# Token-major x, causal row sums from VectorE blocks, and a layer norm folded behind W in an attention kernel

## The chip, the cores and the metric

The kernel runs on one core of one Trainium2 chip. Times are device microseconds (us) of that core. Most executions of one kernel agree within 0.3%. "PE" is TensorE, "PEld" its weight loads, "DVE" VectorE, "ACT" ScalarE, "POOL" GpSimd, "SP" SyncE, "SPq" the order of transfers that SyncE issues. All runs used below are of the fast state.

## The reference, cut to what matters

```python
x = x + conv_attention(group_norm(x))     # causal: q, k, v from x and positions; softmax; times v
t = tokens(x)                             # 8 images x 2304 tokens x 128 channels, fp32
t = t + softmax(xh @ xh.T) @ xh           # xh = layer_norm(t): full attention, scores symmetric
t = t + ffn(layer_norm(t))                # y = sigmoid(batch_norm(W x) + V y), token after token
```

## The kernel before

Each image has six chunks of 384 tokens. A chunk passes through causal attention, a layer norm, full attention, and a second layer norm whose result is multiplied by W; the recurrence runs at the end, for all images. Scores of the full attention are symmetric, so an exponential computed for one block serves for the mirrored one too. VectorE turns it in 32x32 squares into a tile `t`, SyncE stores it in memory as `e` (576 KB) and loads it back as `g` (four transfers of 144 KB), and the product `o<-g` uses it.

What stands behind the causal attention, with the row sums by three products of one column, and x transposed by TensorE:

```python
def sums():                                               # row sums of the causal softmax
    tp = psum_t(f"dn_{b}_{j}")
    for g in range(QB):                                   # QB = 3
        nc.tensor.matmul(tp[:, g : g + 1], acc[:, ts(g, P)], ones[:, 0:1], start=True, stop=True)
    nc.vector.reciprocal(ri, tp[:, :QB])
def residual():
    to = transposed(o_sb, f"oc_t_{b}_{j}")                # three 128x128 transposes by TensorE
    tx = transposed(xbuf[b][:, cols], f"x_t_{b}_{j}")
    nc.scalar.copy(xr, tx[:, :QC])
    ...                                                   # y = to * ri + xr
```

And behind the full attention, where t2 (the sum of the second line, tokens on partitions) is transposed once as it is and once normalized:

```python
(sums, residual, rooted,     # row sums, t2 = o * ri + t1, rs = 1/sigma by GpSimd
 keep,                       # tp = transposed(t2, "tk"), copied to t2c, stored for the end
 normed,                     # x2 = (t2 - mean) * rs       (VectorE)
 back,                       # xc = transposed(x2, "tx")
 statistics)                 # wx = W @ xc; batch-norm statistics
```

Loads of `g` run through three buffers; stores and loads stand in one order of issue, SyncE's.

Of the kernel before, what the change touches and what calls it, by code (L numbers as in the profile page):

```python
# [3 lines left out]

# [9 lines left out]
F32 = mybir.dt.float32  # L14
# [7 lines left out]
NPE = 2 * EMB  # L22
# [524 lines left out]
class Stream:  # L547
# [14 lines left out]
    def then(self, at, ops):  # L562

        for engine, us in ops:
            at = max(at + self.HOP, self.free[engine]) + us
            self.free[engine] = at
        return at + self.HOP
# [33 lines left out]
def fast_path(ctx: ExitStack, tc: tile.TileContext, x, wq, bq, wk, bk, wv, bv, w_ffn, v_ffn, gamma, beta, pe, out, flag):  # L601
# [28 lines left out]

    ident = cpool.tile([P, P], F32, tag="ident", name="ident")
    make_identity(nc, ident)
    ones = cpool.tile([P, P], F32, tag="ones", name="ones")
# [18 lines left out]
    with ExitStack() as actx:  # L652
# [40 lines left out]
        def load_x(b):  # L693
            xbuf[b] = big.tile([P, N], F32, tag="x", name=f"x_{b}")
            for h in range(2):
                nc.sync.dma_start(xbuf[b][:, ts(h, N // 2)], x_v[b, :, ts(h, N // 2)])

        load_x(0)


# [21 lines left out]
        wpT = chunk_tile("t2", "wpT").rearrange("p (j c) -> p j c", j=3)  # L722
        raw = tpool.tile([P, N // 2], F32, tag="t", name="raw")
        wn = [raw[:, ds(j * (C + NPE), C + NPE)] for j in range(3)]
        vn = raw[:, ds(3 * (C + NPE), P)]
        for j, (w, bias) in enumerate(((wq, bq), (wk, bk), (wv, bv))):
            nc.scalar.dma_start(wn[j], w)
            nc.scalar.dma_start(wpT[NPE : NPE + 1, j, :], bias.rearrange("(o c) -> o c", o=1))
            if j == 0:
                nc.scalar.dma_start(pe_sb[0][: NPE + 1, :], pe[:, : N // 2])  # L730
        nc.scalar.dma_start(pe_sb[1][: NPE + 1, :], pe[:, N // 2 :])
        nc.scalar.dma_start(w1, w_ffn)
        nc.scalar.dma_start(vn, v_ffn)
        nc.scalar.dma_start(gb[:, 0:1], gamma.rearrange("(c o) -> c o", o=1))
        nc.scalar.dma_start(gb[:, 1:2], beta.rearrange("(c o) -> c o", o=1))
        for j in range(3):
            tp = psum_t(f"tp_w_{j}")
            nc.tensor.transpose(tp[:, 0:P], wn[j][:, 0:C], ident)
            nc.tensor.transpose(tp[0:NPE, P : 2 * P], wn[j][:, C : C + NPE], ident)
            nc.vector.tensor_copy(wT[:, j, :], tp[:, 0:P])  # L740
            nc.vector.tensor_copy(wpT[0:NPE, j, :], tp[0:NPE, P : 2 * P])

        def ffn_weights():
            tp = psum_t("tp_ffn")
            nc.tensor.transpose(tp[:, 0:P], w1, ident)
            nc.tensor.transpose(tp[:, P : 2 * P], vn, ident)
            nc.vector.tensor_copy(w1T, tp[:, 0:P])
            nc.vector.tensor_copy(vT_f, tp[:, P : 2 * P])


        SQ = 32
        R = P // SQ
        same = apool.tile([P, R, SQ], F32, tag="same", name="same")
        nc.vector.tensor_reduce(same[:, 0, :], ident.rearrange("p (a c) -> p c a", c=SQ), AX.X, ALU.add)
        for r in range(1, R):
            nc.vector.tensor_copy(same[:, r, :], same[:, 0, :])
        mine = apool.tile([P, NQ - 1, R, QB], F32, tag="mine", name="mine")
        nc.vector.tensor_reduce(mine[:, 0, :, 0], ident.rearrange("p (a c) -> p a c", c=SQ), AX.X, ALU.add)
        for i in range(NQ - 1):
            for g in range(QB):  # L760
                if i + g:
                    nc.vector.tensor_copy(mine[:, i, :, g], mine[:, 0, :, 0])
# [45 lines left out]
        pos = {}  # L808

        def load_positions(b, n):  # L810
            if 0 < b < B:
                pos[b, n] = pbp.tile([P, 3, QC], F32, tag="pb", name=f"pb_{b}_{n}")
                nc.sync.dma_start(pos[b, n], posb_d[:, n])

        def project(b, n):
# [4 lines left out]
            def positions(j):  # L820
                def f():
                    if j == 0:
                        c["pb"] = pbp.tile([P, 3, QC], F32, tag="pb", name=f"pb_{b}_{n}")
                    pe_c = pe_sb[n // (NQ // 2)][: NPE + 1, ts(n % (NQ // 2), QC)]
                    ps = psum_s(f"pb_{n}_{j}")
                    if j < 2:
                        nc.tensor.matmul(ps[:, :QC], wpT[: NPE + 1, j, :], pe_c, start=True, stop=True)
                    else:
                        for m in range(0, QC, P):
                            nc.tensor.matmul(ps[:, ds(m, P)], pe_c[:, ds(m, P)], wpT[: NPE + 1, j, :], start=True, stop=True)  # L830
                    nc.scalar.copy(c["pb"][:, j, :], ps[:, :QC])
                    if j == 2:
                        nc.sync.dma_start(posb_d[:, n], c["pb"])

                return f

            def normed():
                if b:
                    c["pb"] = pos.pop((b, n))
# [5 lines left out]
                c["xn"] = chunk_tile("xn", f"xn_{b}_{n}", c, 4 if b else 7)  # L845
                nc.vector.tensor_scalar(c["xn"], xbuf[b][:, cols], mg, rs, ALU.subtract, ALU.mult)

            def part(j):
                def f():
# [14 lines left out]
                    if j < 2:  # L864
                        nc.vector.tensor_reduce(
                            largest[b][:, j, n : n + 1], dst, AX.X, ALU.max, apply_absolute_value=True
                        )
                    else:
                        load_positions(*divmod(b * NQ + n + 2, NQ))
                        if n + 1 < EARLY:  # L870
                            project(b, n + 1)

                return f

            steps = [] if b else [(positions(j), QC * US, [("ACT", 0.5)]) for j in range(3)]
            steps.append((normed, 0.0, [("DVE", 0.75)]))
# [31 lines left out]
        def transposed(src, name):  # L908
            tp = psum_t(name)
            for g in range(QB):  # L910
                nc.tensor.transpose(tp[:, ts(g, P)], src[:, ts(g, P)], ident)  # L911
            return tp

# [5 lines left out]
        class Causal:  # L919
# [57 lines left out]
            def after(self, j, o):  # L977
# [4 lines left out]
                o_sb = chunk_tile("o", f"oc_{b}_{j}", c, 2)  # L982
                nc.scalar.copy(o_sb, o[:, :QC])
                at = st.then(st.now, [("ACT", 0.5)])

                def sums():

                    tp = psum_t(f"dn_{b}_{j}")
                    for g in range(QB):
                        nc.tensor.matmul(tp[:, g : g + 1], acc[:, ts(g, P)], ones[:, 0:1], start=True, stop=True)  # L990
                    ri = small.tile([P, QB], F32, tag="ric", name=f"ric_{b}_{j}")
                    nc.vector.reciprocal(ri, tp[:, :QB])  # L992
                    c["ri"] = ri

                def residual():
                    to = transposed(o_sb, f"oc_t_{b}_{j}")
                    tx = transposed(xbuf[b][:, cols], f"x_t_{b}_{j}")
                    xr = chunk_tile("xr", f"xr_{b}_{j}", bufs=1)
                    nc.scalar.copy(xr, tx[:, :QC])  # L999
                    y = t1p.tile([P, QC], F32, tag="t1t", name=f"t1t_{b}_{j}")  # L1000
                    for g in range(QB):
                        nc.vector.scalar_tensor_tensor(  # L1002
                            y[:, ts(g, P)], to[:, ts(g, P)], c["ri"][:, g : g + 1], xr[:, ts(g, P)], ALU.mult, ALU.add
                        )
                    if j == NQ - 1 and b + 1 < B:
                        load_x(b + 1)
# [14 lines left out]
                def back():  # L1021
# [4 lines left out]
                    (sums, 0.6, [("DVE", 0.2)]),  # L1026
                    (residual, 0.7, [("ACT", 0.5), ("DVE", 2.6)]),
# [5 lines left out]
        class Full:  # L1033
# [3 lines left out]

            def __init__(self, b):
# [3 lines left out]
                self.used = 0  # L1042
# [23 lines left out]

            def prefetch(self):
                n = len(self.loaded)
# [4 lines left out]
            def turned(self, j, m, p, ready):  # L1073
# [3 lines left out]
                if g == 0:  # L1077
                    self.tiles[n] = tpool.tile([P, R, QB, QB, SQ], F32, tag="t", name=f"t_{b}_{j}_{n}")
# [5 lines left out]
                if g == QB - 1:  # L1084
                    d = dpool.tile([P, R, QB * QB * SQ], F32, tag=f"e_{j}_{n}", name=f"e_{b}_{j}_{n}")
                    nc.sync.dma_start(d, t.rearrange("p b j m r -> p b (j m r)"))
                    self.stored[j, n] = d, at
# [8 lines left out]
            def begin(self, j, what, first):  # L1096
# [12 lines left out]
                if what[0] == "turned":  # L1109
                    i, g = what[1:]  # L1110
                    while (i, j) not in self.loaded:
                        self.load()
# [24 lines left out]
            def after(self, j, o):  # L1137
# [5 lines left out]
                at = st.then(st.now, [("ACT", 0.5)])  # L1143

# [23 lines left out]
                def residual():  # L1168
                    tp = transposed(o_sb, f"of_t_{b}_{j}")
                    t2 = chunk_tile("t2", f"t2_{b}_{j}", c, 5)  # L1170
# [5 lines left out]
                    c["mv"], c["ve"] = moments(t2, f"f{b}_{j}", "l2")  # L1176

                def rooted():
                    c["rs"] = root(c["ve"], f"f{b}_{j}", "l2")

                def normed():
                    c["x2"] = chunk_tile("x2", f"x2_{b}_{j}", c, 6)
                    normalize(c["x2"], c["t2"], c["mv"], c["rs"])

                def keep():
                    tp = transposed(c["t2"], f"tk_{b}_{j}")
# [4 lines left out]
                    nc.scalar.copy(self.t2c[:, :, ds(s0, SJ)], tp[:, :QC].rearrange("p (s l) -> p l s", l=LS))  # L1191
# [6 lines left out]
                def back():  # L1198
                    tp = transposed(c["x2"], f"tx_{b}_{j}")
                    c["xc"] = chunk_tile("xc", f"xc_{b}_{j}", c, 7, bufs=1)  # L1200
                    nc.scalar.copy(c["xc"], tp[:, :QC])

                def statistics():
# [5 lines left out]
                c["chain"] = st.add([  # L1209
                    (sums, 0.15, [("DVE", 0.8)]),  # L1210
                    (residual, 0.35, [("DVE", 2.6)]),
                    (rooted, 0.0, [("POOL", 0.9)]),
                    (keep, 0.35, [("ACT", 0.5)]),
                    (normed, 0.0, [("DVE", 1.1)]),
# [197 lines left out]
```

## Time and profile before

The time before is 1854.35 us, the median of three runs (1854.31 to 1856.12).

| quantity | before | where it is read |
|---|---|---|
| span of the profiled run | 1852.4 us | head of the page |
| TensorE busy / idle | 1817.4 / 35.0 us | busy row; span less busy |
| mean granted TensorE clock | 0.993 | list of cores |
| DMA moved; share of SyncE's queue in 16 engines' time | 207.24 MB; 37.5% | DMA part |
| `e<-t` and `g<-e`, issue to landing (median) | 3.2 and 3.7 us | list of DMA issues |
| first score; first score of the full attention | 22.15; 130.16 us | TensorE in order of time |

The table is to be read as follows: TensorE has hardly any idle time left, and DMA has much. A queue's "share" adds up the time during which its packets were under way, on 16 engines. It counts waiting inside a packet like moving, and this will matter.

### The profile page before, as it was taken

How to read it: one execution, taken by the hardware profiler on the slowest of the kernel's cores; microseconds unless marked ns; L12 is line 12 of the kernel's file. 1: busy time of each engine (PE TensorE's matmuls, PEld its weight loads, DVE VectorE, ACT ScalarE, POOL GpSimd, SP SyncE). 2: the span in 40 equal slices, each digit the busy share in tenths (PEclk: the TensorE clock that was granted, in tenths of full speed). 3: DMA queues.
4: the chain of work that ended last, by engine and by line, in shares of the span. 5: the costliest groups of instructions: out<-in, count | busy, mean ns of one | idle time of the engine just before them, and what ended most of it. 6: DMA issues, size and time to landing. Idle time of an engine off the chain costs nothing.

```text
span 1852.4 us, 22328 instructions
## 1 busy us (share of the span) xinstructions
PE 1817.4 (98%) x6885; PEld 1159.6 (63%) x6886; DVE 1218.8 (66%) x3152; ACT 773.5 (42%) x1976; POOL 198.4 (11%) x292
## 2 busy tenths in 40 slices
PE   7999999999999999999999999999999999999987
PEld 4666666666666666666666666666666666666656
DVE  5747667575766667575675757666675756757457
ACT  2345334443345423454244433454234542445346
POOL 1100011000110001100110001100011000200006
PEclk9999999999999999999999999999999999999988
DMA  2105551256303571055511563034720456005667
GB/s 92 51 1 192 155 131 35 79 164 175 76 19 128 152 185 48 1 186 143 150 35 57 159 182 95 22 117 148 190 58 1 165 155 158 9 13 166 181 197 206
DMA packets 176558, 207.24 MB, mean 112 GB/s; under 512 B 85865, under 2 KB 147948, under 8 KB 175662
## 3 DMA queue, kind: packets, MB, share of 16 engines
q1 hardware_dynamic: 174608, 202.42, 37.5%
q0 software_dynamic: 720, 2.62, 0.9%
q8 instruction: 57, 0.93, 0.2%
q10 hardware_dynamic: 1102, 0.68, 0.1%
q14 instruction: 71, 0.58, 0.1%
HBM read 112.49 MB, written 93.19 MB: 111 GB/s over the span
## 4 chain that ended last, share of the span: by engine, by line
PE 96%; DVE 1%; POOL 1%; DMA 1%; issue 1%; ACT 0%; SPq 0%; POOLq 0%; DVEq 0%
PE s L1117 18%; PE o L1131 18%; PE s L948 16%; PE o L959 16%; PE o L1127 13%; PE pj L853 3%; PE pj L856 2%; PE wx L1205 2%; PE dn L990 1%; PE x_t L911 1%; PE tb L911 1%; PE of_t L911 1%; PE tx L911 1%; PE oc_t L911 1%; PE z L1346 1%; PE tk L911 1%
## 5 line engine op out<-in xcount | busy, mean ns | idle before, releaser
L1119 ACT ACTIVATE p<-s,shift 128x384 f32<-128x384 f32 x504 | 293.1, 582 | 448.5 <-PE s L1117 435.4
L1117 PE MATMUL s<-xh 128*128 128x384 f32 x1008 | 410.8, 489 | 0.0
L1131 PE MATMUL o<-p,xhT 128*128 128x384 f32 x1008 | 403.2, 487 | 0.0
L948 PE MATMUL s<-q,k 128*128 128x384 f32 (+2 forms) x1008 | 380.2, 459 | 0.5 <-DVE k L863 0.5
L959 PE MATMUL o<-p,vT 128*128 128x384 f32 (+2 forms) x1008 | 377.0, 456 | 0.0
L950 ACT ACTIVATE p<-s 128x384 f32<-128x384 f32 (+2 forms) x504 | 231.0, 462 | 349.6 <-PE s L948 287.4
L1127 PE MATMUL o<-g,xhT 128*128 128x384 f32 x720 | 279.7, 488 | 0.1
L1131 PEld LDWEIGHTS o<-p,xhT 128*128 128x128 f32 x1008 | 188.0, 190 | 121.3
L959 PEld LDWEIGHTS o<-p,vT 128*128 128x128 f32 x1008 | 188.5, 190 | 114.6 <-issue 0.3
L1117 PEld LDWEIGHTS s<-xh 128*128 128x128 f32 x1008 | 183.7, 190 | 106.8
L974 DVE TENSOR_TENSOR acc<-acc,p 128x384 f32<-128x384 f32 (+2 forms) x408 | 210.1, 515 | 60.0 <-ACT p L950 38.1
L948 PEld LDWEIGHTS s<-q,k 128*128 128x128 f32 x1008 | 178.6, 191 | 88.8 <-DVE acc L974 1.1
L1080 DVE STREAM_TRANSPOSE t<-p 128x384 f32<-128x384 f32 x360 | 187.0, 553 | 45.5 <-ACT p L1119 42.7
L1127 PEld LDWEIGHTS o<-g,xhT 128*128 128x128 f32 x720 | 132.2, 190 | 79.0 <-issue 0.7
L1090 DVE TENSOR_REDUCE tsum<-t 128x12 f32<-128x1152 f32 x120 | 162.3, 1353 | 4.1
L858 DVE TENSOR_TENSOR z<-pj,pb 128x384 f32<-128x384 f32 x144 | 79.2, 550 | 110.2 <-PE pj L853 105.3
L953 POOL TENSOR_TENSOR p<-p,triu 128x128 f32<-128x128 f32 x144 | 72.0, 500 | 447.3 <-ACT p L950 446.4
L901 POOL TENSOR_TENSOR rs_f<-ve_f,mhalf 128x3 f32<-128x3 f32 x48 | 41.5, 865 | 684.7 <-DVE ve_f L895 684.7
L992 DVE RECIPROCAL ric<-dn 128x3 f32<-128x3 f32 x48 | 8.5, 177 | 135.9 <-PE dn L990 135.9
L1119 ACT ACTIVATION_READ_ACCUMULATOR p<-s,shift 128x1 f32 x504 | 97.3, 193 | 0.0
L1002 DVE SCALAR_TENSOR_TENSOR t1t<-oc_t,ric,xr 128x128 f32<-128x128 f32 x144 | 41.6, 344 | 68.3 <-ACT xr L999 67.9
L853 PE MATMUL pj<-xn,wT 128*128 128x384 f32 x192 | 80.3, 504 | 0.0
(249 smaller groups left out, 1595.0 us busy)
## 6 DMA issues: line engine op xcount, KB each, us to landing
e<-t SPq DMA_DIRECT2D x120, 576.0 KB, 3.2
g<-e SPq DMA_DIRECT2D x480, 144.0 KB, 3.7
pb<-posb_d SPq DMA_DIRECT2D x42, 576.0 KB, 3.8
x<-in_x_dram SPq DMA_DIRECT2D x16, 576.0 KB, 4.8
out_dram<-t2s SPq DMA_DIRECT2D x26, 256.0 KB, 3.9
t_d<-t2c SPq DMA_DIRECT2D x16, 384.0 KB, 4.4
t2s<-t_d SPq DMA_DIRECT2D x6, 1024.0 KB, 6.9
posb_d<-pb SPq DMA_DIRECT2D x6, 576.0 KB, 2.8
```

The source lines that it names most:

```text
L853: nc.tensor.matmul(ps[:, :QC], wT[:, j, :], xn, start=True, stop=True)
L911: nc.tensor.transpose(tp[:, ts(g, P)], src[:, ts(g, P)], ident)
L948: nc.tensor.matmul(s[:, off:QC], keys[b][:, ts(m, P)], queries[b, j][:, off:], start=True, stop=True)
L950: nc.scalar.activation(p[:, off:], s[:, off:QC], AF.Exp, scale=SCALE)
L959: nc.tensor.matmul(o[:, off:QC], vals[b][:, ts(m, P)], p[:, off:], start=first, stop=last)
L974: nc.vector.tensor_add(a[:, off:], a[:, off:], p[:, off:])
L1080: nc.vector.transpose(t[:, :, :, g, :].rearrange("p b j r -> p j b r"), p.rearrange("p (j b r) -> p j b r", j=QB, b=R))
L1090: nc.vector.tensor_reduce(self.tsum[j][:, n - j - 1, :], t.rearrange("p b j m r -> p (b j) (m r)"), AX.X, ALU.add)
L1117: nc.tensor.matmul(s[:, :QC], xh[:, ts(m, P)], xh[:, ts(j, QC)], start=True, stop=True)
L1119: nc.scalar.activation(p, s[:, :QC], AF.Exp, bias=shift, accum_out=self.rows[:, m, j : j + 1])
L1127: nc.tensor.matmul(out_ap, xhT[:, QB * i + g, :], p, start=first, stop=last)
L1131: nc.tensor.matmul(o[:, :QC], xhT[:, what[1], :], p, start=first, stop=last)
```

## The change

The intent is to take work off TensorE. (1) The host also lays x token-major, so `x_t` goes. (2) VectorE transposes the sums in 32x32 squares and reduces them; one product of 12 columns and a mask finish the row sums. (3) W's rows are centred once, so the norm's mean falls out, and 1/sigma is multiplied on the product. Then only the raw t2 need be turned: VectorE turns its squares (`tt`), and a round trip through memory (`t2m`, `t2x`) puts the squares in place. 1/sigma, one number per token on the partition of that token, must become a row that every partition sees: it is written to memory (`rs`) and read back by all 128 partitions (`scale`). The last two chunks of the last image keep the old path. (4) Stores of `e` and these transfers are put in SyncE's order when their source is estimated to be ready. (5) The start gets idle products, host-laid weights and another order of positions. The diff, cut:

```diff
 def sums():                                    # causal
-    for g in range(QB):
-        nc.tensor.matmul(tp[:, g : g + 1], acc[:, ts(g, P)], ones[:, 0:1], start=True, stop=True)
+    nc.tensor.matmul(tp[:, :k], same..., c["parts"], start=True, stop=True)     # 12 columns
+    nc.vector.tensor_mul(own..., tp[:, :k], mine...)
+    nc.vector.tensor_reduce(ri, own.rearrange("p a g -> p g a"), AX.X, ALU.add)
 def residual():
-    tx = transposed(xbuf[b][:, cols], f"x_t_{b}_{j}")
...
+def spread():
+    c["rs_d"] = dpool.tile([QB, P], F32, tag=f"rs_{j % 2}", name=f"rs_{b}_{j}")
+    nc.sync.dma_start(c["rs_d"].rearrange("g p -> p g"), c["rs"])
+    c["t2_d"] = dpool.tile([P, QC], F32, tag=f"t2m_{j % 2}", name=f"t2m_{b}_{j}")
+    d = c["t2_d"].rearrange("(k c) (a f) -> a c k f", c=SQ, a=R)
+    for r in range(R):
+        nc.sync.dma_start(d[r], c["tt"][ts(r, SQ)].rearrange("c (k f) -> c k f", k=R))
+def fetch():
+    nc.sync.dma_start(c["t2x"], c["t2_d"])
+    nc.sync.dma_start(c["scale"], c["rs_d"].rearrange("g p -> (g p)").partition_broadcast(P))
+def product():                                  # wx = W' @ t2x, then times scale
...
+steps = [(spread, 0.0, [("", 10.0)]), (fetch, 0.0, [("", 9.0)]), (product, ...), (stored, ...)]
-    d = dpool.tile([P, R, QB * QB * SQ], F32, tag=f"e_{j}_{n}", name=f"e_{b}_{j}_{n}")
-    nc.sync.dma_start(d, t.rearrange("p b j m r -> p b (j m r)"))
+    self.to_store.append((j, n, t, at))         # stored later, when the estimate says ready
...
+for i in range(12):                             # idle products at the start
+    nc.tensor.matmul(tp[:, :P], ident, ident, start=True, stop=True)
```

Note the second line of `spread`. `rs` is a tile of 128 partitions x 3 numbers, and the target is laid out group by group. So each of the 384 numbers is a piece of 4 B of its own, and the pieces of neighbouring partitions lie side by side in memory. This transfer is called the scatter below.

## The prediction

> **What bounds the kernel now.** I read the head of the page, then the chain that ended last, then the order of time on TensorE inside one image, and last the waits.
>
> ```profile
> span 1852.4 us, 22328 instructions
> PE 1817.4 (98%) x6885; PEld 1159.6 (63%) x6886; DVE 1218.8 (66%) x3152; ACT 773.5 (42%) x1976; POOL 198.4 (11%) x292
> PE 96%; DVE 1%; POOL 1%; DMA 1%; issue 1%; ACT 0%; SPq 0%; POOLq 0%; DVEq 0%
> ```
>
> TensorE is busy for 1817.4 of 1852.4 us and carries 96% of the chain. The waits agree: from the second image to the seventh, TensorE waits for nothing longer than 0.3 us. The chain shows the same instruction once an image:
>
> ```profile
> 353.47 0.75 PE s L1117 x2
> 570.90 0.75 PE s L1117 x2
> ```
>
> So an image takes 217.43 us, all of it TensorE's instruction stream; the idle time (35.0 us in all) lies nearly all in the first 66 us (11.8) and after 1776 us. What counts is therefore how much room an instruction takes in that stream. This is read from start to start, because durations overlap. In order of time (start, duration, line):
>
> ```profile
> 1004.40 0.81 PE L1131 MATMUL o<-p,xhT 128*128 128x384 f32 x2
> 1005.04 0.72 PE L990 MATMUL dn<-ones,acc 128*128 128x1 f32 x6
> 1005.63 0.89 PE L1117 MATMUL s<-xh 128*128 128x384 f32 x2
> 1006.36 0.81 PE L1131 MATMUL o<-p,xhT 128*128 128x384 f32 x2
> 1007.00 0.49 PE L911 MATMUL oc_t<-ident,oc 128*128 128x128 f32 x3
> 1007.33 0.49 PE L911 MATMUL x_t<-ident,x 128*128 128x128 f32 x3
> 1007.66 0.81 PE L1117 MATMUL s<-xh 128*128 128x384 f32 x2
> ...
> 1033.37 0.33 PE L1153 MATMUL ts<-tsum,same 128*128 128x60 f32 x2
> 1033.53 0.87 PE L1117 MATMUL s<-xh 128*128 128x384 f32 x2
> 1034.23 0.81 PE L1131 MATMUL o<-p,xhT 128*128 128x384 f32 x2
> ```
>
> A product of 384 columns takes 0.645 us (1004.40 to 1005.04). A group of three transposes takes 0.33 us (1007.33 to 1007.66), though it is shown as 0.49. The row sums `dn` (three products with one column) take 0.59 us, and the product behind them 0.73 in place of 0.645, so 0.67 in all: three weight loads of a full block each for one column of output. One product of the kind `ts` takes 1034.23 - 1033.37 - 0.645 = 0.22 us.
>
> **What the Trainium skill says.** (1) "Perfetto Trace Analysis", Identifying the Most-Contended Engine, holds that matmul busy time is a poor measure of the distance to the roofline. True here too: the groups' own busy times add up to more than the engine's 1817.4 us. I use 98% only together with the absence of waits. (2) "TensorE: Matmul & The Clock Gate", Part 4, gives about 275 ns for a 128x128 transpose in a kernel. The trace has a mean of 273 to 277 ns, but its room in the stream is 0.33 / 3 = 0.11 us, and that is what a removed one returns. (3) "VectorE: DVE Perf Modes", The three transpose paths: VectorE transposes 32x32 blocks only. So the change has to finish the job with a small product and a mask (row sums) or with a transfer (t2). The trace's 128x384 stream transposes take 553 ns. (4) "DMA: Bandwidth & Descriptors", Specifications: transfers reach line rate from 512 B. The change writes t2 in pieces of 384 B and 1/sigma in pieces of 4 B. No line of before isolates that price.
>
> **The change, part by part.** The built programs of both kernels give the counts; there are 8 x 6 = 48 chunks.
>
> - Transposes. `x_t` goes (x now also comes token-major from memory): 48 groups. `tk` and `tx` go for all but the last two chunks, 46 each, because t2 is turned by VectorE and a transfer through memory, and the norm's mean goes into a centred W, its 1/sigma behind the product. 140 x 0.326 = 45.6 us less.
> - Row sums: 48 x 0.67 = 32.4 us go, 48 products of 12 columns come: 48 x 0.22 = 10.6. Net 21.8 us less.
> - Steady sum: 67.4 us. A middle image saves 6 x (3 x 0.326 + 0.67 - 0.22) = 8.6 us, so its period should be 208.9 us.
> - VectorE per chunk: + stream transpose of the sums 0.55, + reduction of 384 about 0.55 (`largest`, same size, 0.553), + mask and small reduction 0.33, + transpose of t2 0.55, + scaling out of PSUM 0.55, - normalization 3 x 0.29 = 0.87. That is +1.66 us, 79 us in all: 1219 becomes about 1295 us, 72% of the new span. Beside TensorE, not on its path.
> - ScalarE loses 48 copies of x_t at 0.48: 23 us less, off the path.
> - Transfers: per chunk 4 writes of 48 KB, a 1.5 KB scatter, and three reads of 192 KB (x, t2, the broadcast scale): 0.77 MB, so about 37 MB on 207. SyncE issues some 370 more (184 + 3 x 46 + 48 + 4). DMA share rises from 38% to perhaps 50%.
> - Start. Before, TensorE starts its first position product at 13.3 us and runs half as fast until about 22 us; the same four instructions:
>
> ```profile
> 13.32 2.92 PE L827 MATMUL pb<-pe,wpT 33*128 33x384 f32 x4
> 23.13 1.55 PE L827 MATMUL pb<-pe,wpT 33*128 33x384 f32 x4
> ```
>
> The first score is at 22.15 us. After, the weights need no transposes, 12 idle products warm the array, and two chunks of positions fill the group norm's wait. Adding the durations of the new order I get the first score at 14 to 16 us. Part of these 7 us is lost again: positions now go to memory and back through one free buffer before the third chunk's VectorE work (a store of 2.8 us and a load of 3.8, one after the other), and products wait for it. I count 4 us net, estimated between 0 and 8.
> - End. The last two chunks keep the old path, so the 77 us from the last `o` to the end should stay.
>
> Without new waits: 1854.35 - 67.4 - 4 = 1783 us.
>
> **The rivals.** (a) VectorE becomes the bound in places. Stretches of 10 us show where it has no room; the columns are the stretch, its length, and busy time of TensorE, its weight loads, VectorE, ScalarE, GpSimd, then clock, DMA share and GB/s:
>
> ```profile
> 1010.00:1020.00 10.00, 10.00 (x35) 5.98 (x34) 9.83 (x20) 5.71 (x17) 0.85 (x1) 1.00 0.74 255
> 1100.00:1110.00 10.00, 10.00 (x40) 6.28 (x39) 6.92 (x14) 2.83 (x8) 0.94 (x1) 1.00 0.99 240
> 1140.00:1150.00 10.00, 10.00 (x46) 6.98 (x45) 9.68 (x31) 3.75 (x9) 2.93 (x6) 1.00 0.17 45
> ```
>
> At 1010 and 1140 VectorE is over 96% busy, and the change adds 1 to 3 us of work there. Against it: just before 1010 VectorE sits idle for 5.3 us waiting for `dn` and 2.4 us for the copied x, and the new work fits into that; six buffers of p give several us of slack. If it bites: 1 to 2 us an image, 8 to 16 us.
> (b) Turned blocks come late. At 1100 DMA is already at 99%, and the loads of `g` run through three buffers:
>
> ```profile
> DMA to landing us min/median/max: 2.5/3.7/5.9
> ```
>
> Four issues (about 1.8 us) and 3.7 us of landing stand against roughly 6 us between a buffer's release and its next use. New stores of t2 and the scatter stand in SyncE's order ahead of such loads, and SyncE waits in order. For it: little slack. Against: before, no product waited for one, and the change places each transfer by an estimate. If it bites: 1 to 3 us an image, 8 to 25 us.
> (c) The round trip of t2 is longer than the 19 us that the schedule allows it, and TensorE waits at `wx`. Two landings of about 4 us stand against it, so I think it unlikely; it would cost some us an image.
> (d) The gain is hidden because something else ends last. The 96% of the chain speak against it.
>
> **Range and chances.** From 1783 I add 8 us for (a) and (b) together, about 1 us an image: 1791 us. If nothing waits and the whole start gain stays, 1854.35 - 67.4 - 8 = 1779; a little below that is possible. If (a) and (b) both bite hard (35 us), and the start gives nothing, 1787 + 35 = 1822; I think 1813 holds the upper tenth. A gain of over 2% needs 1817.3 us: 0.92. Within 2%: 0.06. Slower: 0.02, for a transfer that holds up SyncE's order every image.
>
> **What would show it.** Right: the period of a middle image near 209 to 210 us in the chain; no groups `x_t`, nearly none of `tk` and `tx`; `dn` as 48 small products; TensorE busy near 1750 us; VectorE near 1295; first score near 15 us. (a) would show as idle time of `s` or `o` ended by VectorE or by ScalarE waiting for VectorE; (b) as idle time of the products out of `g` ended by DMA; (c) as idle time of `wx` ended by the loads of t2x or scale. I am wrong if the period falls by clearly less than 8 us, or if the start up to the first full stage is not earlier than before.

## The result, and the profile after

The changed kernel took 1865.04 us (median of four runs, 1861.03 to 1866.10), beside 1854.51 us for the kernel before. The ratio is 1.0051, 95% interval 1.0033 to 1.0068: within 2%, and a little slower. (A ratio is the mean time of one kernel's fast runs over that of the other's fast runs in the same rounds, so it is not quite the ratio of the medians.) 1791 us had been predicted. Head, busy row and shares of the chain after:

```profile
span 1863.2 us, 21869 instructions
PE 1781.9 (96%) x6291; PEld 1106.2 (59%) x6291; DVE 1284.5 (69%) x3275; ACT 780.3 (42%) x1882; POOL 203.0 (11%) x303
...
PE 68%; DMA 16%; DVE 8%; issue 6%; SPq 1%; ACT 0%; POOL 0%; DVEq 0%; ACTq 0%; POOLq 0%
```

The work did go: TensorE has 594 fewer instructions. But it is busy for only 35.5 us less (1817.4 - 1781.9), and idle for 81.3 us instead of 35.0. The chain, which held 96% TensorE, now holds 16% DMA. TensorE's waits (what for: us in total, times, longest) name the transfer:

```profile
PE o L1170 <- DMA g<-e: 33.7, 23, 5.4
PE of_t L923 <- DVE t2x L1249: 10.0, 7, 3.4
...
PE o L1170 <- DMA t2m<-tt: 4.1, 2, 3.3
```

The turned blocks come late. One such place, first in SyncE's order of issue (start, how long the issue took, transfer):

```profile
452.48 0.38 SPq L1232 DMA_DIRECT2D rs<-rs_f  x1
453.10 2.28 SPq L1236 DMA_DIRECT2D t2m<-tt  x4
455.75 10.52 SPq L1094 DMA_DIRECT2D g<-e  x8
```

and then in TensorE's order of time (start, duration, instruction, and in brackets the idle time before it and what ended it):

```profile
456.53 0.81 PE L1170 MATMUL o<-g,xhT 128*128 128x384 f32 x2
462.76 1.62 PE L1170 MATMUL o<-g,xhT 128*128 128x384 f32 x2 [5.42 <-DMA g<-e]
464.17 1.49 PE L1160 MATMUL s<-xh 128*128 128x384 f32 x2
465.45 1.49 PE L1170 MATMUL o<-g,xhT 128*128 128x384 f32 x2
```

TensorE stands for 5.42 us, and then the next products take 1.28 us from start to start (465.45 - 464.17) instead of 0.645. After its idle time a stall is paid for a second time. The Trainium skill, "TensorE: Matmul & The Clock Gate", Part 1, says that an idle array falls to half its clock after an idle window of about 3.4 us and needs some busy microseconds to come back; this trace agrees, with 1.28 against 0.645 us. The chain at that place goes through two transfers (start, duration):

```profile
444.26 7.52 DMA e<-t
...
451.80 10.82 DMA g<-e
```

Before, they took 3.2 and 3.7 us at the median. The engines' share was high in these times, while few bytes moved. Windows of 10 us (busy times of TensorE, weight loads, VectorE, ScalarE, GpSimd, then clock, DMA share, GB/s) of the changed kernel, the first right after `rs` was issued at 390.05 us, the second after the one at 452.48:

```profile
390.00:400.00 10.00, 10.00 (x36) 6.11 (x35) 5.25 (x18) 4.25 (x14) 0.85 (x1) 1.00 0.93 109
...
460.00:470.00 10.00, 7.24 (x19) 4.36 (x20) 2.08 (x8) 0.67 (x2) 0.00 (x0) 0.66 0.78 164
```

At 390 us the 16 engines are 93% occupied with 109 GB/s. The kernel before moved 240 GB/s at 99% in the window from 1100 us that the prediction shows. So something keeps packets under way without moving bytes. DMA as a whole moved 246.23 MB (before 207.24), and SyncE's queue has a share of 58.5% (before 37.5%).

Theories after this reading. T1: the scatter `rs` of 4-byte pieces holds the engines. T2: the writes of t2 in 384-byte pieces do. T3: something else of the change does, such as later stores or more bytes. T4: not the engines but SyncE's order is the trouble, because it stands still at `rs` until GpSimd is done while loads of `g` queue up behind it.

### The profile page after: what moved, and what is told of

Same layout as the page of the kernel before. It is cut to its first block, busy times and chain, and to the rows that moved or that the text cites. A ratio compares the mean times of both kernels' runs of the same rounds, so it can differ in the third digit from the quotient of the medians.

```text
span 1863.2 us, 21869 instructions
## 1 busy us (share of the span) xinstructions
PE 1781.9 (96%) x6291; PEld 1106.2 (59%) x6291; DVE 1284.5 (69%) x3275; ACT 780.3 (42%) x1882; POOL 203.0 (11%) x303
## 2 busy tenths in 40 slices
DMA packets 241940, 246.23 MB, mean 132 GB/s; under 512 B 132913, under 2 KB 212690, under 8 KB 241044
## 3 DMA queue, kind: packets, MB, share of 16 engines
q1 hardware_dynamic: 240860, 241.73, 58.5%
## 4 chain that ended last, share of the span: by engine, by line
PE 68%; DMA 16%; DVE 8%; issue 6%; SPq 1%; ACT 0%; POOL 0%; DVEq 0%; ACTq 0%; POOLq 0%
PE o L983 14%; PE s L972 14%; PE s L1160 12%; PE o L1174 11%; PE o L1170 7%; DMA e<-t 6%; DMA g<-e 5%; PE pj L863 3%; DMA rs<-rs_f 2%; PE z L1457 1%; PE pj L866 1%; DVE t L1123 1%; PE tb L923 1%; DMA scale<-rs 1%; SPq L1094 1%
## 5 line engine op out<-in xcount | busy, mean ns | idle before, releaser
L1160 PE MATMUL s<-xh 128*128 128x384 f32 x1008 | 416.8, 495 | 0.0
L1170 PE MATMUL o<-g,xhT 128*128 128x384 f32 x720 | 294.3, 502 | 41.0 <-DMA g<-e 33.7
L977 POOL TENSOR_TENSOR p<-p,triu 128x128 f32<-128x128 f32 x144 | 76.6, 534 | 522.1 <-ACT p L974 473.4
L913 POOL TENSOR_TENSOR rs_c<-ve_c,mhalf 128x3 f32<-128x3 f32 x48 | 43.8, 913 | 364.7 <-DVE ve_c L907 283.6
L1249 DVE TENSOR_TENSOR t2x<-wx,scale 128x384 f32<-128x384 f32 x46 | 25.0, 544 | 61.6 <-ACT t2c L1272 42.7
```

The costliest lines, as they stand in the source:

```text
L913: nc.gpsimd.tensor_tensor(rs, ve, mhalf, ALU.pow)
L1160: nc.tensor.matmul(s[:, :QC], xh[:, ts(m, P)], xh[:, ts(j, QC)], start=True, stop=True)
L1170: nc.tensor.matmul(out_ap, xhT[:, QB * i + g, :], p, start=first, stop=last)
```

## The experiments

The kernel before ran in the same rounds; its median was 1854.03 us (runs e1 to e4), 1854.28 us (e5 to e8) and 1856.22 us (e9). All twelve kernels gave correct results, and none was refused. A number in brackets is the ratio to before.

**e1_rs_rows: 1/sigma in rows of 128 B**

```diff
+nc.gpsimd.tensor_tensor(rs32[:, :QB], c["ve"], mhalf, ALU.pow)     # rs32: 128 x 32, zero elsewhere
+nc.vector.transpose(c["rsT"], rs32)                                # row a*32+g: 32 tokens of group g
-nc.sync.dma_start(c["rs_d"].rearrange("g p -> p g"), c["rs"])
+for r in range(R):
+    nc.sync.dma_start(c["rs_d"][:, ts(r, SQ)], c["rsT"][r * SQ : r * SQ + QB])
```

> Edit: VectorE turns 1/sigma first, so that its 1.5 KB go to memory in 12 pieces of 128 B (four transfers) instead of 384 pieces of 4 B; all else as in the changed kernel, 1865 us. T1 (the scatter of 4-byte pieces holds the DMA engines for some 7 to 10 us a chunk, and turned blocks come late for it): most of the missing time comes back, 1800 to 1820 us, and the waits of o for g<-e fall from 33.7 us to under 10. T2 (the 384-byte writes of t2 hold the engines) and T4 (the order of SyncE's queue, whatever the sizes): 1855 to 1868 us, waits for g unchanged.

Measured: 1792.71 us (0.966, interval 0.9644 to 0.9676), better than T1's own range. Waits for `g` fell from 33.7 us to 1.0. The busy row and SyncE's queue (packets, MB, share):

```profile
PE 1759.5 (98%) x6291; PEld 1103.8 (62%) x6291; DVE 1290.1 (72%) x3321; ACT 780.1 (44%) x1882; POOL 203.6 (11%) x304
...
q1 hardware_dynamic: 223564, 241.73, 47.4%
```

The same 241.73 MB, the same 6291 instructions on TensorE, but the share is 47.4% instead of 58.5%. Taken off the span, 1090 us of all 16 engines (58.5% of 1863.2) became 850 (47.4% of 1793.1): 240 us for 46 transfers of 1.5 KB, 5.2 us each (an estimate, since other packets that waited meanwhile are counted in it). TensorE's 70.1 us of span split into 47.7 us less idle time (81.3 to 33.6) and 22.4 us less busy time for the same number of instructions. The half rate behind stalls is about 12 us of the latter: span times (1 - mean granted clock) is 39.1 us in the changed kernel (clock 0.979) and 26.9 us in e1 (0.985), an estimate. The rest of the 22.4 us is not explained here. T2 and T3 fall, for their writes and stores are all still there. T4 is unlikely, for SyncE's order waits even longer for 1/sigma here (194.9 us, and 100.0 in the changed kernel) and now issues four transfers in place of one.

One link in the changed kernel is easily missed. What SyncE's own order waited for (us in total, times, longest), in the changed kernel:

```profile
SPq L1094 <- DMA rs<-rs_f: 69.9, 29, 6.3
SPq L1240 <- DMA t2m<-tt: 69.8, 18, 8.5
```

and in e1, where nothing is put down to the landing of `rs`:

```profile
SPq L1248 <- DMA t2m<-tt: 1.7, 6, 0.8
```

So not the wait for 1/sigma, but the slow landings do hold up SyncE's order too: it stands at loads of `g` until `rs`, and at the load of `t2x` until `t2m` has landed.

**e2_old_t2, e3_old_scatter, e4_old_writes: one part at a time**

```diff
-last = b == B - 1 and j >= NQ - 2
+last = True                                  # e2: old path (tk, tx) for all chunks
 def keep_last():
+    nc.sync.dma_start(c["rs_d"].rearrange("g p -> p g"), c["rs"])              # e3 only, unread
+    for r in range(R):                                                         # e4 only, unread
+        nc.sync.dma_start(d[r], c["tt"][ts(r, SQ)].rearrange("c (k f) -> c k f", k=R))
```

> Edit: all chunks take the old path behind the second attention (tk and tx by TensorE, no t2 round trip, no scatter); token-major x and the new row sums stay. If the round trip is the whole of what went wrong: before's 1854.4 less 15.6 us (x_t) less 21.8 us (row sums), less 0 to 4 us of the start, so 1813 to 1817 us and no waits for g. If something else in the change costs the time (later stores of e, the loads of token-major x, positions through memory): 1825 to 1850 us, with waits left.

> Edit: as e2_old_t2, and the 384-piece scatter of 1/sigma is written too, read by nobody. T1: 30 to 60 us more than e2_old_t2, products wait for g<-e. T2 (384-byte writes): within 5 us of e2_old_t2. T4 (SyncE's order): in between, because SyncE waits here too for 1/sigma, but for one transfer of five: 5 to 15 us more.

> Edit: as e2_old_t2, and t2 is turned by VectorE and written in pieces of 384 B (4 transfers of 48 KB), read by nobody, no scatter. T2: 30 to 60 us more than e2_old_t2. T1: within 8 us of e2_old_t2 (VectorE 0.55 us more a chunk, 9 MB more).

Measured: e2 1809.20 us (0.9751), e3 1853.17 us (0.9989), e4 1814.77 us (0.9781). e2 is a little better than expected and has no wait for `g`. The scatter alone adds 44.0 us to it, as T1 said; the 384-byte writes of t2, with VectorE's turning, add 5.6 us. So token-major x, the row sums and the later stores were sound, and the loss hangs on 46 transfers that carry 69 KB together. In the changed kernel they cost 72.3 us (1865.04 - 1792.71), 28 us more than here. There the round trip of t2 stands behind them in SyncE's order as well; that this makes the 28 us is likely from the waits above, but no run separates it.

**e5_scatter_apart and e7_scatter_sbuf: the same pieces elsewhere**

```diff
-c["rs_d"] = dpool.tile([QB, P], ...);     dma_start(c["rs_d"].rearrange("g p -> p g"), c["rs"])      # e3
+c["rs_d"] = dpool.tile([QB, P, P], ...);  dma_start(c["rs_d"][:, :, 0].rearrange("g p -> p g"), ...) # e5
+c["rs_w"] = small2.tile([P, QB, 2], ...); dma_start(c["rs_w"][:, :, 0], c["rs"])                     # e7
```

> Edit: as e3_old_scatter (1853.2 us, against 1809.2 us without the scatter), but every piece of 4 B goes to a place of its own, 512 B from the next, instead of into one stretch of 1.5 KB. T1a (the price is that 384 pieces fall into the same few lines of memory and are done one after the other): within 8 us of 1809. T1b (the price is that of a small write to memory as such): 1840 to 1856 us, as e3_old_scatter.

> Edit: as e3_old_scatter, but the 384 pieces of 4 B go to another place in SBUF instead of memory. T1a and T1b (the price is that of small writes to memory): within 8 us of e2_old_t2, 1809 us. T1c (the price is that of a small piece whatever its target): 1840 to 1856 us.

Measured: e5 1809.66 us (0.976, interval 0.9744 to 0.9776) and e7 1809.16 us (0.9753), both like e2. So T1a holds: 384 pieces of 4 B cost next to nothing, in memory (512 B apart) as in SBUF (three to a partition, 8 B apart), if they do not lie side by side. SyncE's queue and the scatter's median landing time, in e3 (side by side) first:

```profile
q1 hardware_dynamic: 201116, 214.58, 56.5%
...
rs<-rs_f SPq DMA_DIRECT2D x46, 1.5 KB, 10.1
```

and in e5 (512 B apart):

```profile
q1 hardware_dynamic: 201116, 214.58, 41.1%
...
rs<-rs_f SPq DMA_DIRECT2D x46, 1.5 KB, 3.1
```

Packets and bytes are the same to the last digit; only the target addresses differ. This pair also settles T4: SyncE's order waits for 1/sigma just as long in both, in e3

```profile
SPq L1296 <- POOL rs_f L913: 156.9, 14, 14.4
```

and in e5

```profile
SPq L1296 <- POOL rs_f L913: 156.1, 14, 14.4
```

and the times are 43.5 us apart. The Trainium skill, "DMA: Bandwidth & Descriptors", Why small descriptors are slow (HBM only), puts the price of small pieces to memory down to a few cycles and 32 B per piece, and says that transfers within SBUF are free of the penalty. The runs agree that it is small: over e2, e7 adds (0.408 x 1807.6 - 0.403 x 1808.2) / 46 = 0.19 us of all 16 engines a scatter, e5 0.30 us. Side by side it is 6.9 us (e3, the same sum). That is another thing than what the page describes. Nor is it spent in the small pieces: summed over the packet records of the two traces, packets of 4 B took 21.3 us of all 16 engines in e3 and 19.4 in e5, but those of 128 B 215.1 and 60.7, and those of 4608 B 431.6 and 307.2. It is the packets of other transfers that take longer while such a scatter is under way. Where "holds the engines" is said here, this is meant.

**e9: how far apart**

```diff
+c["rs_d"] = dpool.tile([QB, P, k], ...)       # k = 4, 8, 16, 64 numbers: 16, 32, 64, 256 B
```

> Edit: as e3_old_scatter (pieces of 4 B side by side, 1853.2 us, queue share 56.5%) and e5_scatter_apart (512 B apart, 1809.7 us, 41.1%), with the pieces 16 B apart. If the pieces collide in stretches of 64 B: four in a stretch in place of 16, about a quarter of the price, queue share near 45%, 1812 to 1825 us. If they collide in stretches of 512 B: 32 in place of 128 in a stretch, share 45 to 50% likewise; the wider pitches tell the two apart.

> Edit: as e9_pitch16, pieces 32 B apart. Stretches of 64 B: two pieces in each, share near 43%, 1808 to 1814 us. Stretches of 512 B: 16 in each, share 43 to 48%.

> Edit: as e9_pitch16, pieces 64 B apart. Stretches of 64 B: one piece in each, as e5_scatter_apart, share 41%, 1807 to 1811 us. Stretches of 512 B: 8 in each, share 42 to 45%, landing clearly over 3.1 us.

> Edit: as e9_pitch16, pieces 256 B apart. Stretches of 64 B or 256 B: as e5_scatter_apart, share 41%, landing 3.1 us. Stretches of 512 B: two in each, share up to 42%.

Measured (two runs each for e9):

| distance of pieces | time us | queue share | landing of `rs`, median us |
|---|---|---|---|
| 4 B (e3) | 1853.17 | 56.5% | 10.1 |
| 16 B | 1810.95 | 42.1% | 3.7 |
| 32 B | 1810.04 | 41.2% | 3.2 |
| 64 B | 1809.26 | 41.1% | 3.1 |
| 256 B | 1808.57 | 41.1% | 3.0 |
| 512 B (e5) | 1809.66 | 41.1% | 3.1 |
| no scatter (e2) | 1809.20 | 40.3% | - |

My expectation for 16 B was wrong: I had thought the price would fall to about a quarter (45%, 1812 us at least), but nine tenths of it are gone (engine time over e2: 317 us at 4 B, 33 us at 16 B). At 32 B, too, I had expected a little more (43%) than the 41.2% measured. From 32 B on nothing is left to gain. Collisions within stretches of about 32 B, whose price grows faster than the number of pieces in a stretch, would fit these steps; that is inferred. Two small read-modify-writes of one stretch that have to wait for each other would fit too, and the skill's page, in Specifications, speaks of read-modify-write below 512 B; but the stretch inferred here is far shorter than 512 B. Which unit it is, and why eight pieces cost so much more than two, no run here shows.

**e6_rs_by_token: one transfer, 128 pieces of 12 B**

```diff
-c["rs_d"] = dpool.tile([QB, P], ...);  dma_start(c["rs_d"].rearrange("g p -> p g"), c["rs"])
+c["rs_d"] = dpool.tile([P, QB], ...);  dma_start(c["rs_d"], c["rs"])
-... by_block(c["scale"])
+... c["scale"].rearrange("p (a r g) -> p a r g", a=R, g=QB)
```

> Edit: the changed kernel (1865 us), but 1/sigma is written token by token, 128 pieces of 12 B into the same 1.5 KB, and the product reads its scale in that order. T1b (price by the piece): a third of the engines' time for it, about 1.7 us of all 16 engines a chunk instead of 5.2, so few stalls: 1793 to 1810 us. T1a (price by crowding into the same lines): 128 pieces still crowd; 1800 to 1835 us. If the number of pieces did not matter at all: 1860 us.

Measured: 1790.16 us (0.9645, interval 0.9627 to 0.9664), below both ranges, so its time doesn't separate the two; the runs above do. It is the smallest repair: the two dimensions of the target are swapped, and the view that reads them. `rs` lands in 4.2 us, and the queue's share is 49.2%, so 12-byte pieces side by side still cost about 0.7 us of the engines more than e1's rows ((0.492 x 1790.5 - 0.474 x 1793.1) / 46), and slack covers most of that (2.1 us of waits for `g`).

**e8_rows_tail: what was still lost at the start and the end**

In e1's trace TensorE still waited at the very end. In its order of time, TensorE first, then ScalarE:

```profile
1706.91 1.65 PE L1176 MATMUL o<-p,xhT 128*128 128x384 f32 x2 [2.15 <-ACT p L1164]
```

```profile
1705.81 0.48 ACT L1280 COPY t2c<-tk 128x384 f32<-128x384 f32 x1 [3.03 <-DMA t_d<-t2c]
```

The new path hands over chunk 3 later, so its `t2c` is still being stored when chunk 4, on the old path, wants the buffer; ScalarE waits, and an exponential behind it is late.

```diff
 (e1, and)
-last = b == B - 1 and j >= NQ - 2
+last = b == B - 1 and j >= NQ - 3
+for i in range(3):                             # behind the first positions
+    nc.tensor.matmul(tp[:, :P], ident, ident, start=True, stop=True)
```

> Edit: as e1_rs_rows (1792.7 us), with chunk 3 of the last image on the old path too, because there a copy into t2c waited for the store of t2c and held up an exponential (2.15 us of waiting in TensorE at 1706.9 us and half the rate after it), and with three more idle products behind the first positions, where TensorE waited 0.55 us for the group norm and ran at half rate from 9.9 to 19.9 us. If both reasons are right: first score at 15 to 16 us instead of 19.15, no wait at the end, 1783 to 1788 us. If the gap of 0.55 us is not what drops the rate: 1787 to 1790 us. If neither: 1793 us.

Measured: 1785.11 us (0.963, interval 0.9613 to 0.9646), the fastest version here: 69.2 us below before and 79.9 us below the changed kernel. From the last image's first full score to the end it takes 199.0 us (1781.1 - 1582.1), e1 207.2, before 200.2. TensorE's wait of 2.15 us is gone. So the reason for the tail was right. The start is less clear: the first score came at 16.61 us, but with the start untouched it came at 17.23 (e6) to 19.75 us (e9, 16 B), as TensorE's clock fell earlier or later. One trace can't credit the three idle products with that.

## Why the prediction was wrong

**The work removed: right, and hidden.** The prediction had an image at 208.9 us instead of 217.43. With the scatter spread out, the time from one image's first full score to the next is 208.93 us in e1 (540.85 - 331.92). In the changed kernel as it was, such distances lie between 217.1 and 222.3. The row sums and `x_t` alone save 0.326 + 0.67 - 0.22 = 0.776 us a chunk: 217.43 - 6 x 0.776 = 212.8 was implied for e2, and e2 shows 212.5 (341.38 - 128.87, the same score of two images).

**VectorE: right, and rival (a) cost nothing.** 1295 us was predicted and 1284.5 measured. In e1, with 1290.1 us, no wait of TensorE between the start and the last image is put down to VectorE that is longer than 0.5 us. The 8 us allowed for (a) and (b) together were not needed there.

**Rival (b): the right mechanism, with the wrong size; this is the step that failed.** The prediction gave as its reason: "New stores of t2 and the scatter stand in SyncE's order ahead of such loads". It sought the cost in SyncE's order and in bytes: "If it bites: 1 to 3 us an image, 8 to 25 us". The term that was mis-sized stands in "Transfers": the scatter entered as 1.5 KB among 0.77 MB a chunk. Citation (4) named its 4-byte pieces, and the text said that no line isolates that price, and then gave it no term of its own. It measured 72.3 us (1865.04 - 1792.71), 9 us an image. The cost is not its bytes, nor its wait in SyncE's order: with the same pieces 512 B apart (e5) both are unchanged, and the time is e2's. Written side by side, the pieces lengthen the packets of other transfers, by about 5 us of all 16 engines a chunk. SyncE's order was held up as well, as the chance for "slower" had imagined, but as a consequence: by landings that had become slow. The prediction had the share of DMA at perhaps 50%; SyncE's queue had 58.5%, and 47.4% in e1.

**The gain was not off the path; stalls took its place, and cost more than their idle time.** Of the 70.1 us by which the profiled spans of the changed kernel and e1 differ, 47.7 us are idle time and 22.4 us longer busy time, of which TensorE's half rate is about 12 us (the estimate above). The prediction had no term for that. In this pair the loss is nearly half as large again as the waits.

**Rival (c): small, but it came in by another door.** At `wx` TensorE waited for `t2x` once, for 1.6 us. But the 10.0 us of `of_t` shown above, in seven waits, are waits for VectorE's scaling (L1249) on that same path. That scaling's own idle time is put down to the copy of `t2x` (42.7 us), a load of `g` (8.4) and `scale` (7.1). TensorE's waits for it are gone in e1, so they too hang on the scatter.

**The start: smaller than told.** The first score was predicted at 14 to 16 us and came at 19.16, because TensorE ran at half rate (clock 0.50) between 10 and 20 us, in spite of the idle products. The first score of the full attention came 7.0 us earlier (130.16 to 123.15). Five or six causal chunks at 0.776 us explain 3.9 to 4.7 of them, so 2.3 to 3.1 us are the start's; 4 was predicted, between 0 and 8.

**The end: not unchanged.** It had been said that the last chunks keep the old path and the end stays. In e1 the last part is 7.0 us longer than before, though 2.6 us of transposes (4 chunks x 2 x 0.326) should have gone: about 9.6 us. e8 got 8.2 of them back. So e1's 1792.7 us is near the predicted 1791 partly by luck: the 8 us added for (a) and (b) were in truth lost at the end.

## What to carry to other kernels

Count the pieces of a transfer and look where neighbouring pieces land, not only how many bytes it has: a transposing write of 4-byte numbers that lie side by side in memory cost more here (72.3 us) than 140 groups of transposes had been expected to save (45.6 us). When DMA shows a high share with few GB/s, look for the small transfer issued just before, and try the same pieces 32 B apart or in longer rows before touching any schedule. And where the bound engine has no other slack, price a stall together with the half rate that can follow it.

## What the Trainium skill lacked or had wrong

- "DMA: Bandwidth & Descriptors", Specifications and Why small descriptors are slow (HBM only): these sections speak of the size of a piece (512 B, a few cycles, 32 B), not of where neighbouring pieces land, and no page gives a price for small writes side by side in memory. 384 pieces of 4 B added about 6.9 us of all 16 engines when side by side (e3), 0.7 us when 16 B apart, and 0.3 us from 64 B on (e5: 0.30), nearly all of the 6.9 us in packets of other transfers; side by side, transfers in flight lengthened (`e<-t` from 3.2 to 5.0 us at the median, `g<-e` from 3.5 to 5.0, e2 against e3).
- The same page, Specifications: a read-modify-write below 512 B would make one expect a price for 4-byte pieces that are 64 or 256 B apart. In the kernel's time none was seen: 1809.26 and 1808.57 us, against 1809.20 without the scatter; the engines had about 0.3 us more a scatter. The 384-byte writes of t2 cost no more than 5.6 us for 46 chunks (e4), VectorE's part included.
- "TensorE: Matmul & The Clock Gate", Part 1: the half clock was seen, but also after a wait well below the 3.4 us of an idle window. In e1 a wait of 1.45 us (TensorE was busy for 2.03 us of the window 43.60:47.00) ended at 47.08 us, and the next product of 384 columns took 1.44 us from its start to the next one's; in e8 the same wait of 1.45 us ended at 44.90 us, and the same product took 0.75 us. The page says that the window runs freely, which would make the effect of such a wait a matter of luck; the length of a wait alone did not decide it here.
